# Top-2 experts of a sequence kernel: all eight computed densely, or tokens sorted by expert through a DRAM table and only the chosen two computed

## Chip, core and metric

The kernel runs on one core of one Trainium2 chip. The metric is the device time of one launch in microseconds (us). The kernel before has a median of 1132.59 us in three runs (1129.7 to 1134.93).

## What is computed

The input is 8 sequences of 512 tokens with 128 features. Four layers follow one another, each on a layer-normalised copy of the running sum and each added to it. The last one is the subject here.

```python
x = x + _L0_attn_ref(_layernorm(x), ...)   # a scan over time with gates
x = x + _L0_ffn_ref(_layernorm(x), ...)    # one 128 x 128 matrix, the same for all tokens
x = x + _L1_attn_ref(_layernorm(x), ...)   # the delta rule: 16 heads, a scan over time
x = x + _L1_ffn_ref(_layernorm(x), ...)    # 8 experts, top 2
# _L1_ffn_ref
    probs = jax.nn.softmax(xf @ w_router, axis=-1)
    topk_w, topk_idx = jax.lax.top_k(probs, TOP_K)          # TOP_K = 2
    mask = jax.nn.one_hot(topk_idx, NUM_EXPERTS, dtype=xf.dtype)
    weights = jnp.sum(topk_w[..., None] * mask, axis=1)
    h = jax.nn.gelu(jnp.einsum('te,ieh->tih', xf, w1) + b1)  # w1: 8 x 128 x 512
    out = jnp.einsum('tih,ihe->tie', h, w2) + b2             # w2: 8 x 512 x 128
    out = jnp.sum(out * weights[..., None], axis=1)
```

The reference computes all eight experts for each token and gives six of them weight zero. Everything is in float32.

## The kernel before

**Chunks.** Time is cut into 8 chunks of 64 steps. A chunk holds 64 steps of 8 sequences, so 512 tokens, in 4 tiles of 128. The loop at lines 760 to 768 handles chunk g in three parts.

- `before(g)` (line 756) is `ssm` (the gated scan, lines 412 to 485), `linear` (487 to 496) and `delta_in` (501 to 586). `delta_in` makes keys, queries and values, stores them to a scratch table in DRAM (line 543), and prepares small matrices on POOL (lines 550 to 583, the last of them at line 583).
- `delta_rule(g)` (590 to 667) loads keys and queries spread out (`kq`, lines 604 and 605) and then runs 16 blocks of six DVE instructions (lines 622, 623, 625, 630, 631, 636). Each instruction needs the one before. Its outputs go through matmuls at lines 654 and 663.
- `experts(g)` (669 to 753) normalises the tokens, computes the router (683 to 714), and then, expert after expert, four matmuls of 512 columns into the hidden layer (line 728), four gelus on ACT (line 730), sixteen matmuls of 128 columns back (line 742), a multiplication by the weight on DVE (line 750, zero for six of eight experts) and an addition on POOL (line 751). All weights stay in SBUF (`w1_sb`, `w2_sb`, line 158).

**Order of the work.** The program text asks for `before(g+1)`, `delta_rule(g)`, `experts(g-1)` in turn. A scheduler then interleaves them and fixes one order for each engine. Each engine takes its instructions strictly in that order, so an instruction that waits holds up all behind it on the same engine. All ordinary DMAs are issued in order by SP; indirect DMAs by POOL. `experts(g-1)` stands beside `delta_rule(g)` in these orders.

**Buffers that matter.** Most tiles of `before` exist once (`a1` to `a7`, `xT`), so `ssm(g+1)` cannot start in earnest until `delta_in(g)` has read them.

The helper lines that a profile names are 370 to 383 (`statistics`, `normalised`), 390 (transposes), 395 and 402 (projections). Line 290 has two indirect gathers at the start, which take the one chosen matrix of the second layer.

Of the kernel before, what the change touches and what calls it, by code (L numbers as in the profile page):

```python
# [8 lines left out]
F32 = mybir.dt.float32  # L9
U32 = mybir.dt.uint32  # L10
AF = mybir.ActivationFunctionType
ALU = mybir.AluOpType
# [10 lines left out]
NHB = 4  # L23
SQUARINGS = 24
TINY = 1e-30
LN_EPS = 1e-5
# [6 lines left out]
def seq_kernel(  # L33
# [35 lines left out]


    nc = tc.nc
    B, T, D = u.shape
# [3 lines left out]
    NB = N // BL  # L76
    HN = N // 2
    QB = B // 2

# [3 lines left out]
    scanp = ctx.enter_context(tc.tile_pool(name="scan", bufs=2))  # L83
    dram = ctx.enter_context(tc.tile_pool(name="dram", bufs=2, space=bass.MemoryType.DRAM))
    ps_mm = ctx.enter_context(tc.tile_pool(name="ps_mm", bufs=2, space=bass.MemoryType.PSUM))
    ps_st = ctx.enter_context(tc.tile_pool(name="ps_st", bufs=1, space=bass.MemoryType.PSUM))
# [3 lines left out]
    def ctile(shape, name, dtype=F32):  # L90
        return const.tile(shape, dtype, tag=name, name=name)

    def ptile(shape, tag, bufs=1, dtype=F32):
        return pipe.tile(shape, dtype, tag=tag, name=tag, bufs=bufs)

    def stile(shape, tag, dtype=F32):
        return small.tile(shape, dtype, tag=tag, name=tag)


# [4 lines left out]
    def ph_tile():  # L104
        return ps_h.tile([P, N], F32, tag="ph", name="ph")

    def po_tile():
        return ps_o.tile([P, N], F32, tag="po", name="po")
# [11 lines left out]
    def load_x(g):  # L120
        x = ptile([P, NT, D], "x", 2)
        for dst, src in of_sequence(x, g, u):
            nc.sync.dma_start(dst, src)
        return x


    w_both = ptile([P, 2, P], "hid", 2 * NHB)
    nc.sync.dma_start(w_both[:, 0, :], W_in)
    nc.sync.dma_start(w_both[:, 1, :], W_out)
    first_x = load_x(0)  # L130
    wp_raw = ptile([P, 3, D], "hid", 2 * NHB)
    nc.sync.dma_start(wp_raw, Wp.rearrange("(c p) d -> p c d", p=P))

    R_BP, R_AL, R_DB, R_G, R_B, R_QKVB, R_B1 = 0, 3, 4, 5, 6, 7, 11
    n_rows = R_B1 + NE * NHB
    rows = ptile([n_rows, P], "hid", 2 * NHB)
    nc.scalar.dma_start(rows[R_BP : R_BP + 3], bp.rearrange("(c p) -> c p", p=P))
# [19 lines left out]
    nc.sync.dma_start(bout_bc, b_out.partition_broadcast(P))  # L157
    w1_sb = ctile([P, NE, NHB * P], "w1_sb")
    w2_sb = ctile([P, NE, NHB, D], "w2_sb")
    for h in range(2):  # L160
        e = slice(h * NE // 2, (h + 1) * NE // 2)
        nc.sync.dma_start(w1_sb[:, e], w1[e].rearrange("e d f -> d e f"))
        nc.sync.dma_start(w2_sb[:, e], w2[e].rearrange("e (c p) o -> p e c o", p=P))
# [3 lines left out]
    make_identity(nc, ident)  # L167
    ones = ptile([P, P], "hid", 2 * NHB)
    nc.vector.memset(ones, 1.0)
# [21 lines left out]
    iota8 = ctile([P, NE], "iota8")  # L191
    nc.vector.tensor_copy(iota8, iota8i)
    iotapi = ctile([P, 1], "iotapi", U32)
    nc.gpsimd.iota(iotapi, pattern=[[0, 1]], base=0, channel_multiplier=1)
# [44 lines left out]
    def col(r):  # L239
        return cols[:, r : r + 1]  # L240

    dbias = ctile([P, 1], "dbias")
# [69 lines left out]
    a0 = ptile([P, 2, P], "x3")  # L312
    sq_tmp = ptile([P, 2, P], "xne")

# [20 lines left out]
    eye_both = ident.unsqueeze(1).to_broadcast([P, 2, P])  # L335
    cur = ptile([P, 2, P], "part", 2)
    nc.vector.tensor_mul(cur, w_both, over_both(rmax))
    for step in range(SQUARINGS + 1):
        sq = squared(cur)
        cur = a0 if step == 0 else ptile([P, 2, P], "part", 2)  # L340
        if step % 3 == 0:
            nc.vector.tensor_copy(cur, sq)
            trace_of(tr0 if step == 0 else rtr, cur, eye_both)
            nc.vector.reciprocal(rtr, tr0 if step == 0 else rtr)
            nc.vector.tensor_mul(cur, cur, over_both(rtr))
        else:
            nc.vector.tensor_copy(cur, sq)
# [28 lines left out]

    def normalised(src, mv, rstd, part="b"):
        shift = stile([P, NT], "shift" + part)
        nc.vector.scalar_tensor_tensor(shift, mv[:, :, 0], -1.0, rstd, ALU.mult, ALU.mult)  # L379
        xn = ptile([P, NT, D], "xn" + part)  # L380
        for i in range(NT):
            nc.scalar.activation(  # L382
                xn[:, i, :], src[:, i, :], AF.Identity, bias=shift[:, i : i + 1], scale=rstd[:, i : i + 1]
            )
        return xn

    def transposed(xn, psum=mm_tile):
        pt = psum()
        for i in range(NT):
            nc.tensor.transpose(pt[:, i * P : (i + 1) * P], xn[:, i, :], ident)  # L390
        return pt
# [109 lines left out]
    def delta_in(g, x2):  # L501
# [32 lines left out]
        nc.scalar.activation(beta, project(wqkvb[:, 3 * P : 4 * P], nT), AF.Sigmoid, bias=col(R_QKVB + 3))  # L534
        vals = ptile([P, N], "vals", 2)
        nc.scalar.activation(
# [131 lines left out]

    def experts(g, xo, base):

# [4 lines left out]
        nc.vector.tensor_add(x3, pt.rearrange("p (i d) -> p i d", d=D), base)  # L675
        mv, rstd = statistics(x3, "e")
        x3T = ptile([P, N], "x3T")
        nc.vector.tensor_copy(x3T, transposed(normalised(x3, mv, rstd, "e"), po_tile))

# [8 lines left out]
        def over_experts(v):  # L688
            return v.unsqueeze(2).to_broadcast([P, NT, NE])
# [8 lines left out]
        nc.vector.tensor_mul(prob, prob, over_experts(stat))  # L698
        best = stile([P, NT, 8], "best")
        besti = stile([P, NT, 8], "besti", U32)  # L700
        for i in range(NT):
            nc.vector.max(out=best[:, i, :], in_=prob[:, i, :])
            nc.vector.max_index(out=besti[:, i, :], in_max=best[:, i, :], in_values=prob[:, i, :])
        nc.vector.tensor_copy(best, besti)
        chosen = stile([P, 2, NT, NE], "chosen")
        for c in range(2):
            nc.vector.tensor_tensor(
                chosen[:, c],
                iota8.unsqueeze(1).to_broadcast([P, NT, NE]),
                over_experts(best[:, :, c]),  # L710
                ALU.is_equal,
            )
        nc.vector.tensor_add(chosen[:, 0], chosen[:, 0], chosen[:, 1])
        nc.vector.tensor_mul(prob, prob, chosen[:, 0])

        pt = po_tile()
        for i in range(NT):
            nc.tensor.transpose(pt[0:NE, i * P : (i + 1) * P], prob[:, i, :], ident)
        probT = ptile([NE, N], "xne")
        nc.scalar.copy(probT, pt[0:NE, :])  # L720
        acc = ptile([P, NT, D], "acc")
        nc.vector.tensor_add(acc, tokens_out(probT, b2_sb, po_tile), x3)

        def hidden_of(e):
            hidden = []
            for c in range(NHB):
                ph = ph_tile()
                nc.tensor.matmul(ph, lhsT=w1_sb[:, e, c * P : (c + 1) * P], rhs=x3T, start=True, stop=True)  # L728
                hid = ptile([P, N], "hid", 2 * NHB)
                nc.scalar.activation(hid, ph, AF.Gelu_apprx_tanh, bias=col(R_B1 + e * NHB + c))  # L730
                hidden.append(hid)
            return hidden

        following = hidden_of(0)
        for e in range(NE):
            hidden = following
            if e + 1 < NE:
                following = hidden_of(e + 1)
            po = po_tile().rearrange("p (i d) -> p i d", d=D)
            for i in range(NT):  # L740
                for c in range(NHB):
                    nc.tensor.matmul(  # L742
                        po[:, i, :],
                        lhsT=hidden[c][:, i * P : (i + 1) * P],
                        rhs=w2_sb[:, e, c, :],
                        start=(c == 0),
                        stop=(c == NHB - 1),
                    )
            part = ptile([P, NT, D], "part", 2)
            nc.vector.tensor_mul(part, po, prob[:, :, e : e + 1].to_broadcast([P, NT, D]))  # L750
            nc.gpsimd.tensor_add(acc, acc, part)  # L751
        for src, dst in of_sequence(acc, g, out):
            nc.sync.dma_start(dst, src)


    def before(g):
        return delta_in(g, linear(ssm(first_x if g == 0 else load_x(g))))

    ready, done = before(0), None
    for g in range(NG):  # L760
        scratch, vals, planes, base = ready
        if g + 1 < NG:
            ready = before(g + 1)
        xo = delta_rule(g, scratch, vals, planes)
        if done is not None:
            experts(*done)
        done = (g, xo, base)
    experts(*done)


# [51 lines left out]
```

## Time and profile before

| | |
|---|---|
| median of 3 runs | 1132.59 us |
| the profiled execution: its time, and its span from first to last instruction | 1134.05 us, 1132.3 us |
| busy: PE, DVE, ACT, POOL | 830.2, 610.8, 531.3, 413.9 us |
| the chain that ended last, by engine | PE 35%, DVE 30%, POOL 16%, ACT 11%, issue 5% |
| HBM read, written | 40.74 MB, 6.29 MB |
| mean granted TensorE clock | 0.831 |

PE is the matmul engine, PEld its weight loads, DVE, ACT and POOL the vector, scalar and GpSimd engines, SP the engine that issues DMAs. "Busy" is the time in which an instruction of the engine ran. A row of groups gives line, engine, operation, output and inputs, shapes, count, then busy time and mean ns of one, and then idle time ahead of it with what ended that idle time. A float32 matmul is two records. A row of the timeline gives start, duration, engine, line, operation. "To landing" is from the issue of a DMA until its data had arrived.

### The profile page before, as it was taken

Reading aid. Unit: us, or ns where it says so; the run is one execution under the profiler, and the core shown is the slowest. Engines: PE = TensorE matmul, PEld = TensorE weight load, DVE = VectorE, ACT = ScalarE, POOL = GpSimd, SP = SyncE. Lnnn points to the kernel's source line nnn. Section 1 sums busy time; section 2 is a strip of 40 time slices with the busy share of each in tenths; the row PEclk is TensorE's granted clock in tenths of the full one; section 3 lists DMA queues with packets and bytes.
Section 4 is the critical chain, followed back from the end, with each engine's and each line's share of the span. In section 5 each row is a group of like instructions: output and inputs, shape, how many; then the busy total and the mean of one; then the engine's idle time right before and its main releaser. Section 6 shows DMA issues by size and latency. Waiting matters only on the chain.

```text
span 1132.3 us, 11164 instructions
## 1 busy us (share of the span) xinstructions
PE 830.2 (73%) x3731; PEld 542.9 (48%) x3731; DVE 610.8 (54%) x1562; ACT 531.3 (47%) x822; POOL 413.9 (37%) x485
## 2 busy tenths in 40 slices
PE   5453515626689779948995599938994899799897
PEld 3331113313356636734574356624662455656565
DVE  4643276577859439843397419752695239610200
ACT  6202635535385274366635573457426563243331
POOL 3303634736233462243623462244424362201111
PEclk9555857757799889977998699958997699899899
DMA  6000700604300052000700052001600070000000
GB/s 199 0 1 10 176 10 25 151 10 98 79 1 1 19 122 56 1 10 10 177 1 9 10 132 45 10 0 42 136 2 8 1 176 1 10 1 1 10 1 10
DMA packets 25519, 49.84 MB, mean 44 GB/s; under 512 B 3875, under 2 KB 19158, under 8 KB 21366
## 3 DMA queue, kind: packets, MB, share of 16 engines
q1 hardware_dynamic: 24896, 48.98, 18.0%
q8 instruction: 29, 0.48, 0.2%
q14 instruction: 28, 0.23, 0.1%
q0 software_dynamic: 64, 0.13, 0.0%
q10 hardware_dynamic: 502, 0.03, 0.0%
HBM read 40.74 MB, written 6.29 MB: 42 GB/s over the span
## 4 chain that ended last, share of the span: by engine, by line
PE 35%; DVE 30%; POOL 16%; ACT 11%; issue 5%; DMA 1%; POOLq 0%; SPq 0%; ACTq 0%; DVEq 0%
PE ph L728 11%; PE po L742 8%; PE mm L395 4%; DVE st L623 4%; DVE so L622 4%; DVE st L636 3%; DVE st L631 3%; PE ph L330 2%; PE mm L402 2%; DVE part L750 2%; DVE st L630 2%; DVE prod L625 2%; PE po L654 2%; POOL rstdb L374 1%; PE mm L390 1%
## 5 line engine op out<-in xcount | busy, mean ns | idle before, releaser
L728 PE MATMUL ph<-x3T,w_sb 128*128 128x512 f32 x512 | 267.8, 653 | 10.1 <-ACT hid L730 10.0
L730 ACT ACTIVATE hid<-ph,cols 128x512 f32<-128x512 f32 x256 | 173.0, 687 | 209.7 <-PE ph L728 209.5
L742 PEld LDWEIGHTS po<-w_sb,hid 128*128 128x128 f32 x2048 | 240.3, 193 | 32.0 <-issue 26.6
L742 PE MATMUL po<-w_sb,hid 128*128 128x128 f32 x2048 | 240.5, 276 | 0.0
L751 POOL TENSOR_TENSOR acc<-acc,part 128x512 f32<-128x512 f32 x64 | 81.6, 1275 | 319.7 <-DVE part L750 313.0
L728 PEld LDWEIGHTS ph<-x3T,w_sb 128*128 128x128 f32 x512 | 90.4, 204 | 128.0 <-ACT hid L730 83.8
L750 DVE TENSOR_TENSOR part<-po,prob 128x512 f32<-128x512 f32 x64 | 43.9, 685 | 133.2 <-PE po L742 133.2
L622 DVE TENSOR_TENSOR so<-kq,st 128x512 f32<-128x512 f32 x128 | 87.7, 685 | 47.8 <-DMA kq<-scratch 44.1
L382 ACT ACTIVATE xnb<-x,shiftb,rstdb 128x128 f32<-128x128 f32 x96 | 40.2, 482 | 120.9 <-DVE shiftb L379 100.2
L623 DVE TENSOR_REDUCE st<-so 128x32 f32<-128x288 f32 x128 | 84.0, 656 | 3.9
L654 PE MATMUL po<-so,wo 128*128 128x256 f32 x256 | 67.6, 414 | 11.9 <-DVE so L622 10.5
L395 PE MATMUL mm<-a,head_ones 128*128 128x512 f32 x80 | 51.2, 756 | 26.1 <-POOL a L553 21.3
L636 DVE TENSOR_REDUCE st<-st 128x64 f32<-128x320 f32 x128 | 63.7, 498 | 3.9
L654 PEld LDWEIGHTS po<-so,wo 128*128 128x128 f32 x256 | 52.0, 209 | 26.7 <-DVE so L622 10.9
L402 PE MATMUL mm<-wT,a 128*128 128x128 f32 x64 | 15.8, 420 | 58.1 <-POOL a L482 58.1
L390 PE MATMUL po<-ident,xne 128*128 128x128 f32 x32 | 12.4, 455 | 61.6 <-ACT xne L382 61.6
L631 DVE TENSOR_TENSOR st<-kq,st 128x256 f32<-128x256 f32 x128 | 54.7, 427 | 3.7
L395 PE MATMUL mm<-xT,wT 128*128 128x512 f32 x64 | 38.6, 714 | 14.2 <-ACT a L424 12.1
L662 POOL TENSOR_TENSOR planes<-planes,upd 128x256 f32<-128x256 f32 (+1 forms) x64 | 34.4, 567 | 38.4 <-ACT upd L639 38.4
L639 ACT COPY upd<-st 128x128 f32<-128x128 f32 x32 | 8.4, 261 | 80.6 <-DVE st L636 80.6
L395 PE MATMUL mm<-a,wqkvb 128*128 128x512 f32 x64 | 42.3, 770 | 3.8 <-ACT a L518 3.8
L630 DVE TENSOR_REDUCE st<-prod 128x32 f32<-128x128 f32 x128 | 37.5, 293 | 12.2 <-ACT upd L639 7.3
(240 smaller groups left out, 1218.6 us busy)
## 6 DMA issues: line engine op xcount, KB each, us to landing
kq<-scratch SPq DMA_DIRECT2D x32, 1024.0 KB, 10.6
x<-in_L_attn_u_dram SPq DMA_DIRECT2D x64, 32.0 KB, 1.7
w_sb<-in_L_ffn_w_dram SPq DMA_DIRECT2D x2, 1024.0 KB, 7.0
scratch<-qn SPq DMA_DIRECT2D x8, 256.0 KB
scratch<-kn SPq DMA_DIRECT2D x8, 256.0 KB, 2.1
so<-vals SPq DMA_DIRECT2D x16, 128.0 KB, 2.0
out_dram<-acc SPq DMA_DIRECT2D x64, 32.0 KB, 1.6
wqkvb<-in_L_attn_w_qkvb_dram SPq DMA_DIRECT2D x1, 256.0 KB, 3.4
```

The costliest lines, as they stand in the source:

```text
L395: nc.tensor.matmul(pt, lhsT=weights, rhs=xT, start=True, stop=True)
L622: nc.vector.tensor_mul(so_v[:, :, :, ts], kq_v[:, :, :, ts], state)
L623: nc.vector.tensor_reduce(w, so_r[:, :, ts, :], AX.X, ALU.add)
L630: nc.vector.tensor_reduce(u4, prod, AX.X, ALU.add)
L631: nc.vector.tensor_mul(sum_n[:, :, 0:BL].rearrange("p (j b) t -> p j b t", b=B), kq_k[:, :, :, ts], u4.unsqueeze(1).to_broadcast([P, DH, B ...
L636: nc.vector.tensor_reduce(terms(n + 1)[:, :, BL], sum_n, AX.X, ALU.add)
L654: nc.tensor.matmul(pt[:, 0:HN], lhsT=wo, rhs=so[:, (q0 + j) * HN : (q0 + j + 1) * HN], start=(j == 0), stop=False,)
L728: nc.tensor.matmul(ph, lhsT=w1_sb[:, e, c * P : (c + 1) * P], rhs=x3T, start=True, stop=True)
L730: nc.scalar.activation(hid, ph, AF.Gelu_apprx_tanh, bias=col(R_B1 + e * NHB + c))
L742: nc.tensor.matmul(po[:, i, :], lhsT=hidden[c][:, i * P : (i + 1) * P], rhs=w2_sb[:, e, c, :], start=(c == 0), stop=(c == NHB - 1),)
L750: nc.vector.tensor_mul(part, po, prob[:, :, e : e + 1].to_broadcast([P, NT, D]))
L751: nc.gpsimd.tensor_add(acc, acc, part)
```

## The change

Instead of all experts for each chunk, the chunks are collected in groups of 2, 2, 2, 1 and 1 (`GROUPS`). For each chunk, `route` does what the first half of `experts` did. When a group is complete, the new `experts(group)` does this:

1. It counts, by two small matmuls and some twenty small DVE instructions, how many tokens each expert has in the group, and gives each (token, choice) a row in a table, so that the rows of an expert lie together and each expert starts at a multiple of 128. A group of 2 chunks has 23 blocks of 128 rows, a group of 1 has 15 (`blocks_of`): the number that is always enough. There are 3 x 23 + 2 x 15 = 99 blocks in all, whatever the router chose.
2. POOL scatters the normalised tokens into the table `places` in DRAM by indirect DMAs, one for each tile and choice: 16 in a group of 2, 8 in a group of 1.
3. SP loads the table back, 4 blocks at a time; PE transposes them; DVE copies them.
4. For each block, SP loads the expert's `w1` with its bias column (128 x 516 floats) from a DRAM table, `w1b_dram`, at a row that stands in a register; PE does four matmuls of 128 columns, ACT four gelus, PE four matmuls of 128 columns with `w2` at an address from a register. PE and SP read their registers from an SBUF tile, 4 at a time.
5. Results are stored to DRAM, 4 blocks at a time. POOL gathers them back by indirect DMAs, 4 for each chunk and choice, into one buffer (`back`), and DVE adds them to `acc` with the router's weight. Then `acc` is stored.

At the start, `w1` is copied from DRAM to DRAM with its bias columns, and both tables are filled with zeros. To make room, `x` and `vals` have one buffer in place of two. Other tiles change only their place.

```diff
+GROUPS = (2, 2, 2, 1, 1)
...
+    def blocks_of(n):
+        return (2 * n * N - NE) // P + NE
...
+    tables = ctx.enter_context(tc.tile_pool(name="tables", bufs=1, space=bass.MemoryType.DRAM))
...
-        x = ptile([P, NT, D], "x", 2)
+        x = ptile([P, NT, D], "x")
...
-        vals = ptile([P, N], "vals", 2)
+        vals = ptile([P, N], "vals")
...
+    FW = NHB * P + NHB
+    w1b_dram = tables.tile([NE * P, FW], F32, tag="w1b_dram", name="w1b_dram")
+    nc.sync.dma_start(w1b_dram[:, 0 : NHB * P], w1.rearrange("e d f -> (e d) f"))
+    nc.sync.dma_start(
+        w1b_dram[:, NHB * P :].rearrange("(e p) c -> p e c", p=P),
+        cols[:, R_B1:].rearrange("p (e c) -> p e c", c=NHB),
+    )
...
+    for table in places:
+        nc.sync.dma_start(
+            table.rearrange("(j p) d -> p j d", p=P), zeros.unsqueeze(1).to_broadcast([P, MAXB, D])
+        )
...
+        nc.tensor.matmul(totals, lhsT=ones, rhs=taken, start=True, stop=True)
+        nc.tensor.matmul(earlier, lhsT=before_ones, rhs=taken, start=True, stop=True)
...
+        nc.vector.tensor_copy(dest[:, :, 0:nt], destf)
...
+        table = places[len(n_done) % 2]
+        results = dram.tile([MAXB * P, D], F32, tag="results", name="results")
+        for k, (_, x3n, _, _) in enumerate(group["chunks"]):
+            for c in range(2):
+                for i in range(NT):
+                    nc.gpsimd.indirect_dma_start(
+                        out=table[0 : nblk * P, :],
+                        out_offset=bass.IndirectOffsetOnAxis(
+                            ap=dest[:, c, k * NT + i : k * NT + i + 1], axis=0
+                        ),
+                        in_=x3n[:, i, :],
+                        in_offset=None,
+                    )
...
+        def hidden_of(j):
+            j0, i = j - j % 4, j % 4
+            m = min(4, nblk - j0)
+            if i == 0:
+                xb = ptile([P, 4, D], "xb", 2)[:, 0:m]
+                nc.sync.dma_start(xb, table[j0 * P : (j0 + m) * P].rearrange("(j p) d -> p j d", p=P))
+                pt = po_tile()
+                for k in range(m):
+                    nc.tensor.transpose(pt[:, k * P : (k + 1) * P], xb[:, k, :], ident)
+                xbT = ptile([P, N], "xbT", 2)[:, 0 : m * P]
+                nc.vector.tensor_copy(xbT, pt[:, 0 : m * P])
+                ats = of_blocks(mybir.EngineType.PE, where[:, 0, j0 : j0 + m], NHB * P)
+                row_ats = of_blocks(mybir.EngineType.SP, where[:, 1, j0 : j0 + m], P)
+                quads[j0] = xbT, ats, row_ats
+            xbT, ats, row_ats = quads[j0]
+            w1b = ptile([P, FW], "w1b", 4)
+            nc.sync.dma_start(w1b, w1b_dram[bass.ds(row_ats[i], P), :])
+            ph = ph_tile()
+            hid = ptile([P, N], "hid", 3)
             for c in range(NHB):
-                ph = ph_tile()
-                nc.tensor.matmul(ph, lhsT=w1_sb[:, e, c * P : (c + 1) * P], rhs=x3T, start=True, stop=True)
-                hid = ptile([P, N], "hid", 2 * NHB)
-                nc.scalar.activation(hid, ph, AF.Gelu_apprx_tanh, bias=col(R_B1 + e * NHB + c))
+                cs = slice(c * P, (c + 1) * P)
+                nc.tensor.matmul(
+                    ph[:, cs], lhsT=w1b[:, cs], rhs=xbT[:, i * P : (i + 1) * P], start=True, stop=True
+                )
...
+            for c in range(NHB):
+                nc.tensor.matmul(
+                    po[:, i * P : (i + 1) * P],
+                    lhsT=hid[:, c * P : (c + 1) * P],
+                    rhs=w2_f[:, bass.ds(at + c * P, P)],
+                    start=(c == 0),
+                    stop=(c == NHB - 1),
+                )
...
+            if i == m - 1:
+                yb = ptile([P, 4, D], "yb")[:, 0:m]
+                nc.vector.tensor_copy(yb, po[:, 0 : m * P].rearrange("p (j d) -> p j d", d=D))
+                nc.sync.dma_start(results[j0 * P : (j0 + m) * P].rearrange("(j p) d -> p j d", p=P), yb)
...
-            part = ptile([P, NT, D], "part", 2)
-            nc.vector.tensor_mul(part, po, prob[:, :, e : e + 1].to_broadcast([P, NT, D]))
-            nc.gpsimd.tensor_add(acc, acc, part)
...
+        for k, (g, _, best, acc) in enumerate(group["chunks"]):
+            for c in range(2):
+                back = ptile([P, NT, D], "back")
+                for i in range(NT):
+                    nc.gpsimd.indirect_dma_start(
+                        out=back[:, i, :],
+                        out_offset=None,
+                        in_=results[0 : nblk * P, :],
+                        in_offset=bass.IndirectOffsetOnAxis(
+                            ap=dest[:, c, k * NT + i : k * NT + i + 1], axis=0
+                        ),
+                    )
+                for i in range(NT):
+                    nc.vector.scalar_tensor_tensor(
+                        acc[:, i, :], back[:, i, :], best[:, i, c : c + 1], acc[:, i, :], ALU.mult, ALU.add
+                    )
...
+    def after(g, xo, base):
+        nonlocal group
+        route(g, xo, base, group)
+        if len(group["chunks"]) == group["n"]:
+            experts(group)
+            if g + 1 < NG:
+                group = new_group(GROUPS[CH[g + 1]])
...
         if done is not None:
-            experts(*done)
+            after(*done)
         done = (g, xo, base)
-    experts(*done)
+    after(*done)
```

## The prediction

> **What bounds the kernel now.** First the page: busy times, slices, costliest groups.
>
> ```profile
> PE 830.2 (73%) x3731; PEld 542.9 (48%) x3731; DVE 610.8 (54%) x1562; ACT 531.3 (47%) x822; POOL 413.9 (37%) x485
> ...
> PE   5453515626689779948995599938994899799897
> ...
> L728 PE MATMUL ph<-x3T,w_sb 128*128 128x512 f32 x512 | 267.8, 653 | 10.1 <-ACT hid L730 10.0
> L742 PE MATMUL po<-w_sb,hid 128*128 128x128 f32 x2048 | 240.5, 276 | 0.0
> L751 POOL TENSOR_TENSOR acc<-acc,part 128x512 f32<-128x512 f32 x64 | 81.6, 1275 | 319.7 <-DVE part L750 313.0
> ```
>
> The experts' matmuls are 508 of PE's 830 us: PE looks like the bound. Next, busy time by stage (columns: stretch, length, PE, PEld, DVE, ACT, POOL, granted clock, DMA share, GB/s): two chunks without experts, one chunk of the steady state, the end.
>
> ```profile
> 90.00:250.00 160.00, 69.84 (x168) 37.17 (x168) 90.98 (x224) 72.86 (x117) 76.50 (x91) 0.64 0.29 68
> 510.00:635.00 125.00, 98.13 (x454) 63.30 (x452) 72.70 (x181) 66.33 (x102) 50.73 (x58) 0.87 0.19 45
> 990.00:1132.00 142.00, 128.28 (x688) 86.93 (x688) 20.76 (x73) 50.61 (x75) 21.51 (x18) 0.93 0.02 4
> ```
>
> A chunk without experts takes some 76 us, with them 125. Why, the DVE timeline tells. Line 527 ends the key norm of `before(g)`; call its start K(g). Line 422 begins the scan's nonlinear part; call it S(g).
>
> ```profile
> 128.13 0.75 DVE L422 TENSOR_SCALAR a<-mm,dbias 128x512 f32<-128x512 f32 x1 [14.42 <-PE mm L395]
> 188.05 0.69 DVE L527 TENSOR_SCALAR a<-mm 128x512 f32<-128x512 f32 x1 [2.09 <-PE mm L395]
> ...
> 535.55 0.69 DVE L527 TENSOR_SCALAR a<-mm 128x512 f32<-128x512 f32 x1 [3.82 <-PE mm L395]
> 554.89 0.69 DVE L622 TENSOR_TENSOR so<-kq,st 128x512 f32<-128x512 f32 x1 [12.30 <-DMA kq<-scratch]
> 602.02 0.74 DVE L422 TENSOR_SCALAR a<-mm,dbias 128x512 f32<-128x512 f32 x1
> 656.25 0.69 DVE L527 TENSOR_SCALAR a<-mm 128x512 f32<-128x512 f32 x1 [2.08 <-PE mm L395]
> ```
>
> S to K is a serial chain over ACT, DVE, POOL and PE: 59.9 us at the start, 54.2 here. K(4) to S(5) is 66.5: 19.3 until `kq` is there, then 47.1 of delta rule, *with the experts beside it on PE*. So a chunk is chain plus delta rule; experts fill time that the delta rule takes anyway. Only the end has experts alone (chain of waits):
>
> ```profile
> 1002.96 3.57 PE po L742 x32
> 1006.53 3.62 PE ph L728 x8
> ```
>
> One expert is 7.2 us, a chunk 58, and two chunks are left there.
>
> **What the Trainium skill says.** "DMA: Bandwidth & Descriptors", section on the anatomy of a DMA on the GpSimd path: about 2 us fixed, most of it the wait until the last byte is confirmed, worst for HBM. "Perfetto Trace Analysis", section on the GpSimd DMA instruction: its recorded end is the end of descriptor generation, not of the transfer. The trace agrees: 1.0 and 1.2 us recorded for the two gathers of line 290, but 5.6 and 4.8 to landing.
>
> ```profile
> bsel<-in_L_ffn_b_dram,b_row POOLq DMA_INDIRECT x1, 5.6
> wsel<-in_L_ffn_W_dram,w_row POOLq DMA_INDIRECT x1, 4.8
> ...
> scratch<-kn SPq DMA_DIRECT2D x8, 256.0 KB, 2.1
> ...
> out_dram<-acc SPq DMA_DIRECT2D x64, 32.0 KB, 1.6
> ```
>
> "TensorE: Matmul & The Clock Gate", part 1: an idle PE is throttled. The clock column agrees (0.64 sparse, 0.93 dense).
>
> **The change, part by part.** I read the order of the built kernel's instructions on each engine and what each waits for. Four facts decide:
> (a) Each scatter waits until the previous one has *landed* (they write one table): 16 or 8 links in a row, in POOL's queue, ahead of POOL's steps of the next `before`.
> (b) On DVE the block copies of groups 0 and 1 stand after the last delta instruction of chunk 3 (or 5) and before the first of chunk 4 (6); on PE the blocks stand inside `delta_in(4)` (6). So blocks no longer run beside a delta rule.
> (c) Group 2's last scatter stands behind the last planes product of chunk 7 on POOL: its 23 blocks start after the last delta rule.
> (d) Groups 3 and 4 are routed only after the group before: their scatters and blocks follow one another.
>
> *A block.* 8 matmuls of 128 columns at 3.57/16 = 0.223 us: 1.79. Transposes 0.15 (line 674, four in 0.60). Register loads are not in this trace; "Runtime: NRT & Kernel Launch", instruction fetch, gives some 200 ns a register: 0.2 a block. An address instruction ahead of each of four matmuls: between 0 (hidden behind the matmul) and 0.2 each; I take 0.08, so 0.32. A clock near 0.9 and short waits: 0.35. Sum 2.8 us. Bounds: 2.2 (registers hidden, full clock; no gain possible, the matmuls stay) and 3.6 (clock 0.64). Hidden: gelu, four at some 0.36 (0.687 for 512, less 384 x 0.86 ns, the slope between the copies of lines 666 and 584), 1.45 < 2.8; the `w1` load, 256 KB like `kn`'s 2.1 us, four buffers ahead. Where `kq` (four of 1 MB, 10.6 us each) shares the queue in groups 0 and 1, that cover goes: +10 us a group (0 to 20). SP has result stores among the `w1` loads: block 7's load waits behind the store of blocks 0 to 3, lands some 4.3 us after block 3, and PE has 5 us of work until it needs it: covered, barely.
>
> *A scatter link.* At least 1.1 + 1.6 = 2.7 (recorded issue, small store); at most 5.8 (the 5.6 above, beside heavy loads, and a handover). I take 4.0.
>
> *A quarter of the gathers* (one chunk, one choice): four issues 4.4, last landing 2.4 later, DVE 1.2: 8 (6.5 to 10). The next needs the same buffer.
>
> *Startup.* `w1` goes to DRAM, 3 MB of zeros are stored, ahead of the loads of chunk 1 on SP. Zeros can start at 81 us (end of the power iteration), 15 us at the 199 GB/s of slice 1; chunk 1 is needed near 100. Nothing, up to 5 us if that cover fails. Single buffers of `x`, `vals`: nothing, refills are asked for early.
>
> *Removed*: 508 us of PE, 44 of DVE, 82 of POOL. In the middle this was beside the delta rule, so little returns; at the end it returns.
>
> *Sum* (times of this execution; S to K taken as 58):
> - K(2) = 265.5, as before. The order now has 89 delta instructions and the first routing ahead of S(3): delta rule 2 begins at 291, then 51 of these (24 us) and 8 of routing: S(3) = 324, K(3) = 382 (404 before).
> - Stage with scatters: delta rule at K+19, routing and ranking among it, S at K+38, K+96 next. Table places ready at K+42. The 13th link must have started before POOL gets to the second norm of `delta_in`: K + 42 + 12 x 4 = K+90. From there 12 us to line 527 (POOL 2.8, then 9.5 as from the end of line 509 at 103.5 to 113.0): K+102. So K(4) = 484.
> - Group 0: the 16th lands at K(3)+106, load, transposes, copy 4.5, 23 x 2.8 = 64, kq 10: ends at K(3)+185 = 567.
> - Then delta rule 4. POOL finishes `delta_in(4)` (8.5 us), first gather lands at 13, DVE has 42 delta instructions and 12 us more ahead of S(5), with waits for four quarters of gathers: 57 (POOL has the gathers behind it by then, so its first step of `ssm(5)`, 8.5 us after S, is not late). S to K 58. K(5) = 682, so two chunks cost 300, not 250.
> - Again: K(7) = 982.
> - Group 2: places at K+41, 16 links 64, 5, blocks 64: 1156 (delta rule 7 ends at K+75, covered).
> - Group 3: store 3.5, two quarters 16, third's issue 4.4, routing 10 (983.9 to 994.9 before is 11, its statistics done early), ranking 6, 8 links 32, 5, blocks 42: 119, so 1275.
> - Group 4: routing 12.5, ranking 6, 32, 5, 42: 97.5, so 1372.
> - End: 3.5, two quarters 16, add and output 5.5: 1397 against a span of 1132.3.
>
> The profiled execution took 1134.05 for that span and the median is 1132.59, so the median stays at about 1398.
>
> **Rivals.**
> 1. *Dear links*: a scatter takes 5.6 us as the startup gathers did. Longer chain 64 x 1.6 = 102 (32 links in the two stages, 16, 16): 1500. For it: the only measured values. Against: they shared the DMA engines with megabyte loads.
> 2. *Cheap links and blocks*: 3 us and 2.4 us, quarters of 7. Links then hide behind K+96 in the middle. 99 x 0.4 = 40, links 51, gathers 12, kq 10: 1285. For it: stores land in 1.6.
> 3. *Faster: freed PE time comes off the path.* If PE bounds the kernel as its slices say, 461 us of dense experts (8 x 57.6) become 99 x 2.8 = 277: 1134 - 184 = 950. For it: PE's nines, 35% of the chain. Against: fact (b), and S to K unchanged by PE's load. It decides from the point where blocks run beside the delta rule and scatters are hidden, over 265 us less than my sum.
> 4. *The change does not do what it says*: the block count is fixed, 99 of 256 tile equivalents, so the work does fall.
>
> **Numbers.** Mine, with link 3.4 to 4.8: 60%, 1398. Rival 1 and dearer: 17%. Rival 2: 17%. Rival 3: 4%; no change 2%, where gain and loss cancel. Within 0.5% is about what cannot be told from no change. Faster 0.04, same 0.02, slower 0.94. Range 1270 to 1515: rivals 1 and 2 inside, and the bounds of block and link but not all together.
>
> **What would show it.** Scatter starts 3.4 to 4.8 us apart on POOL; 2.2 to 3.6 us a block; no delta rule instruction during blocks of groups 0 and 1; K(7) near 982 and the last delta rule ending near 1057, then some 340 us with DVE almost idle. I am wrong if blocks and delta rule overlap, if scatters do not wait for landing, or if register loads cost several us.

## The result, and the profile after

The changed kernel takes 1267.12 us in the median of four runs (1264.54 to 1269.26), the kernel before 1132.3 in four runs beside them: 1.119 times as long, 95% interval 1.1156 to 1.1223. Slower was forecast, but 1398 us, and the range ended at 1270. The profiled execution took 1269.26 us, with a span of 1267.5.

The page, the rows that answer to those of before (busy times, slices, groups):

```profile
PE 598.9 (47%) x2874; PEld 444.1 (35%) x2874; DVE 616.0 (49%) x1696; ACT 446.3 (35%) x942; POOL 459.1 (36%) x552
...
PE   5445165155354238755254047935251098238173
...
L869 POOL DMA_INDIRECT places<-xne,dest x64 | 65.2, 1018 | 157.5 <-DMA places<-xne,dest 69.4
...
L911 PE MATMUL ph<-xbT,w1b 128*128 128x128 f32 x792 | 109.6, 290 | 16.2 <-DMA w1b<-w1b_dram 12.1
L949 POOL DMA_INDIRECT back<-results,dest x64 | 61.6, 962 | 132.5 <-DMA results<-yb 97.0
L933 PE MATMUL po<-w_sb,hid 128*128 x792 | 109.4, 283 | 0.2
```

The experts' matmuls fell from 508 to 219 us and PE from 830 to 599, yet the kernel is 135 us longer: no engine is busy half of the time. POOL idles 69 us waiting for one scatter before the next (line 869). By stage (columns as before): the two chunks without experts, K(3) to K(4), the blocks of group 0, and all after K(7).

```profile
90.00:250.00 160.00, 69.07 (x168) 36.54 (x168) 91.56 (x227) 72.98 (x117) 76.47 (x91) 0.65 0.33 81
372.57:476.72 104.15, 36.69 (x99) 19.75 (x98) 61.66 (x178) 38.14 (x63) 55.12 (x62) 0.60 0.28 71
481.03:543.94 62.91, 49.59 (x390) 47.66 (x391) 8.89 (x17) 33.05 (x102) 12.13 (x16) 0.89 0.75 192
922.80:1267.50 344.70, 158.07 (x1071) 141.82 (x1069) 97.47 (x305) 85.37 (x256) 87.98 (x100) 0.68 0.33 91
```

The first stretch is as before. In the third, DVE works 8.9 of 62.9 us: from 483 us on no DVE instruction of a delta rule runs beside the blocks, as fact (b) of the prediction has it. The DVE timeline of that stretch shows it line by line (line 684 is the last of a delta block's six instructions, 900 the copy of transposed rows, 942 that of results):

```profile
482.74 0.50 DVE L684 TENSOR_REDUCE st<-st 128x64 f32<-128x320 f32 x1
496.85 0.69 DVE L900 COPY xbT<-po 128x512 f32<-128x512 f32 x1 [13.61 <-PE po L898]
497.74 0.69 DVE L942 COPY yb<-po 128x512 f32<-128x512 f32 x1 [0.20 <-PE po L933]
...
543.94 0.56 DVE L942 COPY yb<-po 128x384 f32<-128x384 f32 x1 [4.69 <-PE po L933]
```

The other side of it is in POOL's waits from 481 to 552 us (what waits, for what, us in total, times, longest) and in PE's timeline:

```profile
POOL a L622 <- ACT a L617: 47.0, 1, 47.0
```
```profile
543.74 2.90 PE L443 MATMUL mm<-a,head_ones 128*128 128x512 f32 x6
```

Line 443 here makes the last projections of `delta_in(4)`. They stand in PE's queue behind group 0's blocks and start when the blocks end, at 543.7. ACT's copies of them and then POOL's products (line 622) wait for that, and delta rule 4, which starts at 555.4, with them. So the blocks did not merely lose their cover: they hold up the chain that every chunk runs through (`a_noblock` below shows by how much).

The markers K (line 575 now, 527 before) and S (line 470): K(3), K(4), S(5), K(5) and K(7), and last K(7) of before:

```profile
372.57 0.69 DVE L575 TENSOR_SCALAR a<-mm 128x512 f32<-128x512 f32 x1 [4.49 <-PE mm L443]
476.72 0.69 DVE L575 TENSOR_SCALAR a<-mm 128x512 f32<-128x512 f32 x1
595.28 0.75 DVE L470 TENSOR_SCALAR a<-mm,dbias 128x512 f32<-128x512 f32 x1 [1.24 <-PE mm L443]
650.08 0.69 DVE L575 TENSOR_SCALAR a<-mm 128x512 f32<-128x512 f32 x1 [3.48 <-PE mm L443]
...
922.80 0.69 DVE L575 TENSOR_SCALAR a<-mm 128x512 f32<-128x512 f32 x1 [5.17 <-PE mm L443]
```
```profile
906.71 0.69 DVE L527 TENSOR_SCALAR a<-mm 128x512 f32<-128x512 f32 x1 [4.70 <-PE mm L395]
```

K(7) is at 922.8 (906.7 before), and from there to the end it is 344.7 us (225.6 before). The end gives 119 of the 135 us, the middle 16.

### The profile page after: what moved, and what is told of

Read it like the earlier page. It is cut to its first block, busy times and chain, and to the rows that moved or that the text cites. A ratio compares the mean times of both kernels' runs of the same rounds, so it can differ in the third digit from the quotient of the medians.

```text
span 1267.5 us, 10848 instructions
## 1 busy us (share of the span) xinstructions
PE 598.9 (47%) x2874; PEld 444.1 (35%) x2874; DVE 616.0 (49%) x1696; ACT 446.3 (35%) x942; POOL 459.1 (36%) x552
## 5 line engine op out<-in xcount | busy, mean ns | idle before, releaser
L916 ACT ACTIVATE hid<-ph,w1b 128x128 f32<-128x128 f32 x396 | 110.6, 377 | 103.5 <-issue 42.7
L869 POOL DMA_INDIRECT places<-xne,dest x64 | 65.2, 1018 | 157.5 <-DMA places<-xne,dest 69.4
L911 PE MATMUL ph<-xbT,w1b 128*128 128x128 f32 x792 | 109.6, 290 | 16.2 <-DMA w1b<-w1b_dram 12.1
L949 POOL DMA_INDIRECT back<-results,dest x64 | 61.6, 962 | 132.5 <-DMA results<-yb 97.0
L933 PE MATMUL po<-w_sb,hid 128*128 x792 | 109.4, 283 | 0.2
L911 PEld LDWEIGHTS ph<-xbT,w1b 128*128 128x128 f32 x792 | 100.5, 202 | 20.1 <-DMA w1b<-w1b_dram 13.1
L933 PEld LDWEIGHTS po<-w_sb,hid 128*128 128x128 f32 x792 | 101.3, 200 | 2.9 <-issue 2.1
L443 PE MATMUL mm<-a,head_ones 128*128 128x512 f32 x80 | 54.8, 813 | 36.8 <-POOL a L601 31.6
L898 PE MATMUL po<-ident,xb 128*128 128x128 f32 x99 | 17.9, 301 | 107.8 <-DMA xb<-places 107.8
L438 PE MATMUL mm<-ident,xnb 128*128 128x128 f32 x64 | 23.9, 440 | 91.9 <-ACT xnb L430 91.7
L702 PEld LDWEIGHTS po<-so,wo 128*128 128x128 f32 x256 | 54.8, 220 | 29.7 <-DVE so L670 11.7
L958 DVE SCALAR_TENSOR_TENSOR acc<-back,best,acc 128x128 f32<-128x128 f32 x64 | 25.5, 404 | 62.8 <-DMA back<-results,dest 62.8
```

The costliest lines, as they stand in the source:

```text
L443: nc.tensor.matmul(pt, lhsT=weights, rhs=xT, start=True, stop=True)
L702: nc.tensor.matmul(pt[:, 0:HN], lhsT=wo, rhs=so[:, (q0 + j) * HN : (q0 + j + 1) * HN], start=(j == 0), stop=False,)
L869: nc.gpsimd.indirect_dma_start(out=table[0 : nblk * P, :], out_offset=bass.IndirectOffsetOnAxis(ap=dest[:, c, k * NT + i : k * NT + i + 1] ...
L911: nc.tensor.matmul(ph[:, cs], lhsT=w1b[:, cs], rhs=xbT[:, i * P : (i + 1) * P], start=True, stop=True)
L916: nc.scalar.activation(hid[:, cs], ph[:, cs], AF.Gelu_apprx_tanh, bias=w1b[:, NHB * P + c : NHB * P + c + 1])
L933: nc.tensor.matmul(po[:, i * P : (i + 1) * P], lhsT=hid[:, c * P : (c + 1) * P], rhs=w2_f[:, bass.ds(at + c * P, P)], start=(c == 0), stop ...
```

## The experiments

Each kernel's median, and in its profiled execution K(7) and what follows it, all in us:

| kernel | median | K(7) | K(7) to end |
|---|---|---|---|
| before | 1132.3 | 906.7 | 225.6 |
| after | 1267.1 | 922.8 | 344.7 |
| before, 4 experts (`b_half`) | 1002.1 | 820.6 | 179.4 |
| before, no experts (`b_none`) | 844.5 | 718.9 | 124.9 |
| before, experts emitted early (`b_early`) | 1079.8 | 864.4 | 212.5 |
| after, fixed addresses (`a_static`) | 1268.4 | 924.1 | 342.7 |
| after, a quarter of the w1 loads (`a_fewload`) | 1258.2 | 911.2 | 344.2 |
| after, independent scatters (`a_nowaw`) | 1164.7 | 850.3 | 310.3 |
| after, experts emitted early (`a_early`) | 1208.6 | 862.2 | 344.8 |
| both of these (`a_nowaw_early`) | 1128.4 | 830.3 | 298.9 |
| after, blocks left out (`a_noblock`) | 1021.2 | 804.7 | 214.7 |
| both, blocks left out (`ae_noblock`) | 982.3 | 759.1 | 223.1 |
| both, gathers late (`ae_lategather`) | 1141.3 | 834.1 | 300.9 |
| both, groups of one (`ae_g1`) | 1166.2 | 890.4 | 275.5 |

### What dense experts cost: half of them, none of them

```diff
-        for e in range(NE):
+        for e in range(NE // 2):
...
```


> The kernel before with experts 0 to 3 alone; the other four of eight are left out of the sum. Theory of the prediction (experts lie beside the delta rule and cost time only at the end): the two chunks left at the end have 4 x 7.2 us less each, 58 us, and K to K in the middle stays near 125 us: about 1075 us. Rival (the experts' time on PE is on the path of every chunk, so the change started from something worth saving): five middle chunks come down from 125 towards the 76 us that a chunk without experts takes, half of it 25 us each: about 950 us. If the rival holds, the sorted kernel lost more than 135 us, since it gave up that saving as well.

Measured 1002.1 us (ratio 0.8848, 0.8808 to 0.8888), between the two. The end gave 46 us, the middle 86; K to K fell to 110 to 113. So dense experts did not only fill time that the delta rule takes anyway.

```diff
-        following = hidden_of(0)
-        for e in range(NE):
+        for e in range(0):
```


> The kernel before with no experts at all: routing and the b2 part stay, the eight experts' matmuls, gelus, products and sums are left out. It sets the floor that any way of computing experts stands on. Half of the experts gone gave 132 us (1134.5 to 1002.1), of which 58 at the end. Theory (experts are on the path of every chunk, in the middle too): the other 58 us of the end go, and some 5 x 10 us of the middle: about 895, between 860 and 930. Rival (with half the experts the middle is already down to chain plus delta rule, so nothing more comes there): 1002 - 58 = 944.

Measured 844.5 us (0.7436, 0.7387 to 0.7485), below both. K to K is 86 to 94 us here (lines of the DVE timeline, K(4), S(5) and K(5)), where before had 121 and more:

```profile
452.54 0.69 DVE L527 TENSOR_SCALAR a<-mm 128x512 f32<-128x512 f32 x1 [0.64 <-PE mm L395]
```
```profile
483.89 0.75 DVE L422 TENSOR_SCALAR a<-mm,dbias 128x512 f32<-128x512 f32 x1 [0.62 <-PE mm L395]
```
```profile
538.74 0.69 DVE L527 TENSOR_SCALAR a<-mm 128x512 f32<-128x512 f32 x1
```

S to K is 54.8 us here, as in before (54.2), but K(4) to S(5) is 31.4 where before had 66.5. So the next scan need not wait for the whole delta rule: the 66.5 us, which the prediction read as a wait for `kq` and the delta rule's own time, were stretched by the experts (the scheduler's order may differ as well).

This is the floor, in the order of before. Dense experts cost 288 us above it, 188 of the profiled execution's before K(7) and 101 after; the sorted ones 423.

### Registers, and the bytes of w1

In `a_static` block j uses expert j mod 8 at fixed addresses, for `w1` and `w2`, and not the router's choice; in `a_fewload` four blocks share one load of `w1`, so that three of the four use another expert's first layer.

```diff
-                ats = of_blocks(mybir.EngineType.PE, where[:, 0, j0 : j0 + m], NHB * P)
-                row_ats = of_blocks(mybir.EngineType.SP, where[:, 1, j0 : j0 + m], P)
+                ats = [(j0 + k) % NE * NHB * P for k in range(m)]
+                row_ats = [(j0 + k) % NE * P for k in range(m)]
...
```


> The changed kernel with fixed weights: block j takes expert j mod 8, so no register is loaded and no address instruction stands ahead of a matmul; which expert a block uses is no longer the reference's choice. The order on DVE is that of the changed kernel. Theory (registers hidden; a block in the quiet took 1.92 us, where 8 matmuls alone are 1.79): within 1%, 1255 to 1270. Rival (addressing by register costs 0.2 us a register and 0.08 us an address instruction on the path, as the prediction's block had it): 99 x 0.5 = 50 us less, about 1217.

```diff
-            w1b = ptile([P, FW], "w1b", 4)
-            nc.sync.dma_start(w1b, w1b_dram[bass.ds(row_ats[i], P), :])
+            if i == 0:
+                w1b = ptile([P, FW], "w1b", 4)
+                nc.sync.dma_start(w1b, w1b_dram[bass.ds(row_ats[i], P), :])
+                quads["w1b"] = w1b
+            w1b = quads["w1b"]
```


> The changed kernel with one load of w1 rows for every four blocks, so 25 loads of 258 KB in place of 99 (19 MB less); three of four blocks use the wrong expert's first layer. Theory (the loads are four buffers ahead and hidden): 0 to 12 us less (12 us is all that the first-layer matmuls were seen to wait for these loads), 1255 to 1267. Rival (the doubled DMA traffic, the loads' contention with kq above all, is what makes the kernel slow): blocks of groups 0 and 1 fall from 2.6 to 1.9 us, 2 x 23 x 0.7 = 32 us, and kq arrives earlier: 1225 or less.

Measured 1268.4 and 1258.2 us (ratios to before 1.1178, 1.113 to 1.1226, and 1.1104, 1.1059 to 1.115; the changed kernel has 1.119). Addressing by register costs nothing that can be measured, so the rival of the first text is out. A quarter of the loads saves 9 us: the blocks of group 0 take 52.9 in place of 62.9 us, those of group 1 52.9 in place of 58.0, and those of group 2, where no `kq` shares the queue, 46.6 in place of 47.9. That is the contention that the prediction put at 10 us a group. These loads left out are 19 of the 51 MB by which the DMA traffic grew; what the rest of it costs was not tested by itself.

### Scatters that don't wait for one another

```diff
+                    tc.declare_no_dep(sc, group=f"sc{len(n_done)}", reason="rows are distinct")
+                    tc.add_to_no_dep_group(f"sc{len(n_done)}", sc)
+                    scatters.append(sc)
...
+                for sc in scatters:
+                    tc.add_manual_dep(ld, sc.name, ...)
```


> The changed kernel, with the scatters of a group declared independent of one another (their rows are distinct) and the loads of the table waiting for all of them. Theory (serial links): a link falls from 2.5 to 2.9 us to the 1.0 to 1.1 us of an issue; at the end 41 + 20 + 20 us of scatters become 18 + 9 + 9, so 46 us less; each scatter stage loses up to 37 us. Built, this kernel's order also has the block copies among the instructions of a delta rule, not between two: if the cover is what was lost, another 40 us or so per pair of chunks. Together about 1267 - 46 - 2 x 40 = 1140, between 1100 and 1180. Rival (what costs is the work of the blocks itself, registers and weight loads, or the doubled DMA traffic): the 46 us of the end alone, about 1220, and blocks no shorter.

Measured 1164.7 us (1.0287, 1.024 to 1.0333), 102 less than the changed kernel, and in the range of the theory, though not divided as it had it. In the profiled executions 72 us of it come by K(7), 34 after it (the theory had 80 and 46). POOL's timeline of group 3, first in the changed kernel, then here:

```profile
1117.01 0.97 POOL L869 DMA_INDIRECT places<-xne,dest  x1 [1.53 <-DMA places<-xne,dest]
1119.51 0.97 POOL L869 DMA_INDIRECT places<-xne,dest  x1 [1.53 <-DMA places<-xne,dest]
```
```profile
1022.21 0.97 POOL L870 DMA_INDIRECT places<-xne,dest  x1 [0.30 <-issue]
1023.49 0.97 POOL L870 DMA_INDIRECT places<-xne,dest  x1 [0.31 <-issue]
```

A link is 2.5 us when it waits for landing and 1.27 when it doesn't. The scheduler's order changed too (block copies now lie among delta instructions), so the 72 us of the middle are links and order together.

### Experts emitted ahead of the delta rule, in three kernels

```diff
-        xo = delta_rule(g, scratch, vals, planes)
         if done is not None:
             after(*done)
+        xo = delta_rule(g, scratch, vals, planes)
```

In `b_early` the line in the middle is `experts(*done)`.

> The changed kernel, complete, with one line of the main loop moved: routing and experts of the chunk before are emitted ahead of the delta rule and not after it. Scatters stay in a serial chain. Built, the order has the blocks of groups 0 and 1 between S and K of the next chunk, group 2's among the delta instructions of chunk 7, and group 3's ahead of the last delta rule's end is not there: groups 3 and 4 follow the delta rule. Theory (half of the loss is cover: blocks stood between two delta rules with nothing beside them): some 60 us per pair of chunks less is hidden again, and group 2 leaves the end, 100 us; the chain of scatters stays: 1130, between 1080 and 1180. Rival (the serial scatters are all; order changes nothing, since DVE works in order and delta instructions now stand behind blocks that wait): 1240 to 1270.

> The changed kernel, complete, with both: independent scatters, and routing and experts emitted ahead of the delta rule. Built, the order has block copies among delta instructions in every group but the last. Theory (the loss is two things, serial links and lost cover, which add): K(7) near 372 + 2 x 220 = 812, then a delta rule with groups 2 and 3 beside it, some 140 us, and one group of one chunk alone, 12.5 + 6 + 9 + 5 + 32 + 3.5 + 14 + 5 = 87: about 1040, between 1000 and 1090, so faster than the kernel before. Rival (DVE works in order, so delta instructions behind a waiting block copy lose what the end wins): no better than the independent scatters alone, 1165, or worse.

> The kernel before with the same line moved: experts of the chunk before emitted ahead of the delta rule. A control: how much of what the moved line gives has nothing to do with sorting. Theory: chunk 6's experts lie beside delta rule 7 in place of after it, so one of the two expert passes left at the end, 58 us, goes: about 1075; the middle as before. Rival (the middle gets worse, because part products stand among the delta instructions and wait for PE): 1130 or more.

Measured 1208.6 (1.0649, 1.0583 to 1.0714), 1128.4 (0.9952, 0.9936 to 0.9969) and 1079.8 us (0.9528, 0.9471 to 0.9584). Each theory had the sign, none the place, and both kernels that sort came out between theory and rival. In `a_early` K(7) comes 61 us earlier, but 26 of it had come by K(3) (346.3), before any block ran, and each pair of chunks gave 17 and not 60. The end stays at 345: all of delta rule 7 now stands behind group 2's blocks, which end at 985 us. In `a_nowaw_early` K(7) is 830 and not 812, and the end 299, not 227. In `b_early` the sum came out near 1075, but the middle gave 42 us and the end 13. The moved line helps dense experts (53 us) about as much as sorted ones (59, or 36 where the scatters are independent already): it is no merit of sorting. With both repairs, sorting costs 284 us above the floor; dense experts with the same moved line 235. The floor itself was not measured with the moved line.

### The detour by itself

All DMAs but those of `w1` stay.

```diff
-        following = hidden_of(0)
...
+        for j0 in range(0, nblk, 4):
...
+            nc.vector.tensor_copy(yb, xb)
```

> The changed kernel with the blocks' computing left out: routing, ranking, scatters in their serial chain, the loads of the table and the gathers stay, but a block's result is a copy of its rows (no weight load, transposes, matmuls or gelus). It prices the detour through DRAM by itself, above the 844.5 us of the kernel without experts. Theory (blocks stood alone, so their 62.9 + 58.0 + 47.9 + 32.5 + 32.2 = 233 us of the trace go, less some 5 x 6 us for copying): 1267 - 203 = 1064, so the detour alone is some 220 us, three quarters of what dense experts cost altogether (288). Rival (the blocks were the cost, and the detour hides behind the delta rule once they are gone): below 950.

> The same left out of the kernel with independent scatters and experts ahead of the delta rule (1128.4 us). Theory (here the detour is mostly hidden in the middle, and what is left above the floor is the last group alone, some 12.5 + 6 + 9 + 10 + 14 + 5 = 57, and POOL's time for issues): about 910, between 890 and 940. So some 210 of the 284 us that this kernel has above the floor would be blocks, about what 99 of them last. Rival (the detour's waits on POOL are what stretches the middle): above 1000.

Measured 1021.2 (0.9001, 0.8959 to 0.9043) and 982.3 us (0.8654, 0.8612 to 0.8696). The changed kernel's 423 us above the floor are thus 177 of detour (ranking, scatters, loads, gathers), which stay without blocks, and 246 that go with the blocks and their `w1` loads. In `a_noblock` K(4) to K(5) falls from 173.4 to 115.9 us and K(6) to K(7) from 168.7 to 108.6: about as long as the blocks lasted there (62.9 and 58.0), so they did hold up the chain. The first theory took the detour for some 220 us, 43 more than measured. The second fell: even with independent scatters and the early order the detour costs 138 us, not some 65; the end, 223 us against 125, is most of it.

### What holds the middle: gathers on POOL, or blocks on PE

In `a_nowaw_early`, K(3) to K(4) is 155 us, K(4) to K(5) 89. `ae_lategather` puts group 0's and 1's gathers behind POOL's last step of the next `delta_in`.

```diff
+                    tc.add_manual_dep(
+                        ga,
+                        last_step[-1].name,
...
-            experts(group)
+            late = experts(group)
```

> The kernel with independent scatters and experts ahead of the delta rule, complete, with the gathers of groups 0 and 1 put behind POOL's last step of the next chunk's delta_in. In the trace of that kernel the 16 gathers of group 0 stand on POOL from 458 to 486, between the scan's last POOL step (440) and the steps of linear and delta_in, and K(4) is at 502, so S to K is 130 us and not 55. Theory (gathers in POOL's queue hold up the chain): K(4) and K(6) come 25 to 30 us earlier each: about 1072. Rival (the chain is held by PE and ACT, whose queues have its matmuls and activations behind blocks; the gathers only fill the wait): 1115 to 1130.

Measured 1141.3 us (1.007, 1.0036 to 1.0104): the rival's side, and above its range. K(4) came 13 us earlier (488.9), K(5) not at all (590.4 in both). One thing that holds the chain is seen in `a_nowaw_early` itself; POOL's timeline, then PE's:

```profile
440.20 1.20 POOL L530 TENSOR_TENSOR a<-a,z 128x512 f32<-128x512 f32 x1 [1.38 <-DVE z L521]
```
```profile
452.32 1.95 PE L944 MATMUL po<-w_sb,hid 128*128 x16
454.10 3.62 PE L702 MATMUL po<-so,wo 128*128 128x256 f32 x16
...
463.41 1.07 PE L450 MATMUL mm<-wT,a 128*128 128x128 f32 x8
```

The scan's last product is ready at 441.4, its matmuls (line 450) start at 463.4, behind blocks and the delta rule's output in PE's queue. But blocks are only about half of it: with them left out (`ae_noblock`) K(3) to K(4) still takes 122 us, where this kernel has 155 and the floor 93. One wait of the detour shows there, of the scan's step on ACT for a product that stands in POOL's queue behind 16 scatters:

```profile
ACT a L474 <- POOL a L299: 15.0, 1, 15.0
```

What else makes up the detour's share was not taken apart. The last kernel asked whether shorter runs of blocks help.

```diff
-GROUPS = (2, 2, 2, 1, 1)
+GROUPS = (1,) * 8
```


> The kernel with independent scatters and experts ahead of the delta rule, complete, in eight groups of one chunk: 8 x 15 = 120 blocks in place of 99. In the kernel with groups of two, PE had 23 blocks in its queue from 391 to 450 us, and the scan's output matmuls of the next chunk, ready near 441, started at 460 behind them. Built, the order here has 15 blocks in every chunk, partly among its delta instructions, and chunk 6's beside delta rule 7, so only one group stands alone at the end. Theory (shorter runs of blocks hold the chain up less, and the end loses a group): K to K some 117 us, K(7) near 264 + 5 x 117 = 849, then 75 of delta rule, 40 of group 6 and 87 of the last group: 1050, between 1020 and 1090, which would be faster than both kernels and than dense experts with the same moved line (1080). Rival (21 more blocks of 2 us and a round trip through DRAM in every chunk cost more than that): 1130 to 1180.

Measured 1166.2 us (1.0263, 1.0233 to 1.0294): the rival again. The end lost 23 us, but K to K is 125 to 129 from K(3) on, with PE busy 74 to 76 us of it. Which wait makes up those 127 us was not taken apart further; that stays open.

## Why the prediction was wrong

The direction and the serial mechanism held; the step that failed is the size of two terms of the sum, the block and the scatter link. Both were too large, and the range was too short at that end. The prediction's times beside the trace's:

| step | predicted | measured | of the 130 us too many |
|---|---|---|---|
| K(3) | 382 | 372.6 | 9 |
| K(3) to K(4), K(5) to K(6): scatter stage | 102 | 104.2, 104.1 | -4 |
| K(4) to K(5), K(6) to K(7): blocks, then S to K | 198 | 173.4, 168.7 | 54 |
| K(7) to end of group 2 | 174 | 140.4 | 34 |
| group 3 | 119 | 100.5 | 18 |
| group 4 | 97.5 | 82.2 | 15 |
| end | 25 | 21.6 | 3 |

- *Facts (a) to (d)* all hold: scatters wait for landing, blocks of groups 0 and 1 stand between two delta rules, group 2's blocks run from 1015 us, after delta rule 7's end at 1002.4, and groups 3 and 4 follow in turn.
- *The block* is the first mis-sized term: 2.8 us taken, 2.2 at least. In the quiet, four blocks lie 7.74 us apart (DVE's copies of group 2):

```profile
1033.58 0.69 DVE L900 COPY xbT<-po 128x512 f32<-128x512 f32 x1 [6.16 <-PE po L898]
1041.32 0.69 DVE L900 COPY xbT<-po 128x512 f32<-128x512 f32 x1 [6.15 <-PE po L898]
```

  That is 1.93 us a block, the prediction's own 1.79 for matmuls and 0.15 for transposes; the 0.2 for register loads, 0.32 for address instructions and 0.35 for clock and waits were all nothing. `a_static` shows the first two. Even the lower bound of 2.2 kept 0.26 us that none of its terms explains. The price the prediction took from the Trainium skill ("Runtime: NRT & Kernel Launch", instruction fetch mechanics, some 200 ns a register) is stated there for a load that the page describes as one from HBM; here the registers come from an SBUF tile, and no such cost shows on PE. The mean clock over group 2's blocks was 0.93. The five groups' blocks took 62.9, 58.0, 47.9, 32.5 and 32.2 us where 74, 74, 64, 42 and 42 were summed (contention with `kq` included): 62 us of the 130.
- *The link* is the second: 4.0 us taken, 2.7 at least. It is 2.5 to 3.0 us where nothing else runs (4 for the first of a group): the chain of waits counts 2.24 us from the start of a scatter's issue to its landing. The lower bound had added POOL's recorded 1.1 us to a store's 1.6, but the recorded time lies inside the landing time. The Trainium skill's 2 us fixed for a DMA on the GpSimd path ("DMA: Bandwidth & Descriptors", the anatomy) was the better guide, and agrees. Group 2's 16 links took 43.5 us against 64, groups 3 and 4 some 23 each against 32, groups 0 and 1 some 58 against 64. Of this the sum felt 37 us: the stretches ahead of the blocks, which hold the links, came out 5 us shorter in groups 0 and 1 together, and 17, 9 and 6 us in the others.
- *Contention with `kq`*, 10 us a group: right in size (`a_fewload`: 10 and 5 us from the `w1` loads alone).
- *Scatter stages, startup, S to K* (54.8 against 58), *end of blocks to S(5)* (51 against 57), *a quarter of gathers* (7.1 against 8): right or slightly high. With K(3) (9 us) and the end (3), end of blocks to S and S to K make up the remaining 30 us or so.
- *"Experts fill time that the delta rule takes anyway"*: wrong, though it moved no number of the sum, which was built from the changed kernel's order. The prediction read 47.1 of the 66.5 us from K(4) to S(5) as delta rule that experts merely fill; `b_none` shows that dense experts stretched each chunk in the middle from 86 to 94 us to 121 and more, between K and the next S. Rival 3 had a true core: there was up to 288 us to win. Sorting spent more than that on the detour (177) and on blocks, many of them in the chain's way (246).
- *The rivals*: rival 2 (link 3 us, block 2.4, quarters of 7, 1285 us) is nearest to what happened. It took 50 us off blocks and contention where 62 came off. The range took the bounds of block and link "not all together" at the low end. Over a whole group in the quiet a block came to 2.1 to 2.2 us and a link to 2.7 to 2.9, so both came out at their lower bounds (2.2 and 2.7) at once.

## What to carry to other kernels

What work taken off an engine is worth is shown by a run without it, and the order of instructions decides who gets that time: here 23 blocks in one stretch of PE's queue held a serial chain for 47 us, and the detour took its share, so fewer matmuls made a longer kernel. The scatters into one table formed a chain of landings until they were declared independent, and with that and the moved line sorting came out even with dense experts (1128.4 against 1132.3 us); the dense kernel with the moved line alone beat both (1079.8). When a sum is made of small allowances for things that the trace doesn't show, put the lower bound at what remains with all of them at nothing.

## What the hardware showed that was not expected

- Matmuls whose address comes from a register, four in a block with their address instructions, ran as closely as those with fixed addresses: 99 blocks with and without differ by 1.3 us in 1267.
- A scatter of 128 rows of 512 bytes lands 2.24 us after its issue began (changed kernel, groups 3 and 4), for 0.97 of which POOL is busy; with several in flight POOL issues one every 1.27 us (`a_nowaw`).
- While blocks ran, the granted clock was 0.89 to 0.97, though the changed kernel's mean is 0.678 and the stretch K(3) to K(4) just before the first blocks had 0.60. PE was busy 35% of that stretch and 79 to 98% of the blocks' stretches. Among these the clock did not rise with the share: 0.97 at 82% (group 1), 0.93 at 98% (group 2), 0.90 at 97% (groups 3 and 4).
